# Which TensorE products release the row gathers of a graph layer: those of the small stages and of the picks, or those of the picks alone

## The chip, the cores and the metric

One Trainium2 chip, one NeuronCore of it. The metric is the device time of the whole kernel in microseconds (us). The kernel before takes 1808.46 us, the median of three runs (1806.99 to 1809.7).

## The reference, cut to what matters

200,000 edges, sorted by their target node, join 6,250 nodes of 64 features. Every edge takes the row of its source node, weighs it by nine numbers that a small network makes of its 32 attributes, and the weighted outer products go through `W_tp` and are summed over the edges of each target. A gate made of `node_vec`, the residual and a layer norm end it.

```python
src, dst = edge_index[0], edge_index[1]
w = silu(edge_attr @ W1 + b1) @ W2 + b2                 # 32 -> 64 -> 9, per edge
h_src = features[src]                                   # 64 numbers per edge
msg = einsum('ef,em,fmg->eg', h_src, edge_sh * w, W_tp) # 64 per edge
agg = segment_sum(msg, dst, num_segments=N) / sqrt(E / N)
x = layernorm(x + agg * (1.0 + gamma) + beta)           # gamma, beta from node_vec
```

## The kernel before, in words

The edges lie in 98 blocks (`NBLK`) of 16 tiles of 128 edges. For each block, `hs[g]` (128 x 16 x 64) must be filled with the 128 source rows of each of its tiles. This is done in two ways:

- **Gathers.** An indirect DMA that GpSimd (POOL) issues (line 125) fetches the 128 rows of one tile from DRAM. A block has 12 of them, every fourth block 11, because one tile of it comes row by row over SP's queue (line 143). There are 1148 gathers.
- **Picks.** The other four tiles of a block (three in the first and the last block, five in two of them) are picked out of a copy of `x` that stays in SBUF: VectorE (DVE) makes seven one-hot matrices `hot_k` (line 653), TensorE (PE) multiplies them with the high and the low part of `x` in 14 products into one of three PSUM banks `pxw` (line 668), and DVE takes the right one of seven columns out of it (`xm`, line 678) and sums it into `hs` (line 681). There are 392 picks.

The code is scheduled by hand: a step `i` runs, on PE, pick 0 of block i+1, then the **small stages** (the function `middle`), then picks 1 to 3 of block i+1. The small stages are `hidden(i+2)` (line 594), `second(i+1)` (line 618), in odd steps `project` (line 760), which has ten more products, and `windows(i)` (line 708), which multiplies `hs[i]` with the weighted window matrix `a`. In odd steps two products named `ps` (line 775, function `place`) stand behind the first two and four products of pick 0; ScalarE (ACT) copies half of their bank to `carry` (line 781), DVE adds the other half to the last `carry` (`yt`, line 784), and `second` writes the same PSUM bank next, so it waits for `yt`.

**What sets the times of the gathers.** POOL does nothing but gathers once the setup is done, and takes them in program order. What holds a gather back is a hand-made dependency on a product of PE ("its turn"): in step i the 12 gathers of block i+2 (`LEAD = 2`) are handed out. `beats` sets how many units of PE work a step has and spreads the block's gathers over them evenly; each `beat(units, mm)` behind a product adds that product's units, and a gather that has come due waits for this very product:

```python
def beats(g, units):
    pace.update(g=g, done=0.0, every=units / max(1, len(due[g])))
    pace["next"] = pace["every"] / 2

def beat(units, mm):
    pace["done"] += units
    while due[pace["g"]] and pace["done"] >= pace["next"]:
        gather(pace["g"], len(due[pace["g"]]), mm)
        pace["next"] += pace["every"]
```

A product of a pick counts 1 unit, so a step has 2 * J * 4 = 56 units of picks (J = 7); the small stages count 4.5 (`hidden`), 3.4 (`second`), 12 (`project`) and four times 3.3 (`windows`), and the step's sum is 56 + 21 or 56 + 33. The rows of block i+2 are first read by `windows(i+2)`, two steps later. A gather also waits for the one eight places before it to land.

Of the kernel before, what the change touches and what calls it, by code (L numbers as in the profile page):

```python
# [28 lines left out]
LEAD = 2  # L29
LB = 2  # L30
Q = 5
J = 7
# [20 lines left out]
def picked(g):  # L53

    return Q - 2 if g in (0, NBLK - 1) else Q - (g % 40 != 30)


def tiles(g):
    return min(KB, NT - g * KB)
# [9 lines left out]
def gnn_resnorm_kernel(ctx: ExitStack, tc: tile.TileContext, x, src, dst, dst_row, ea, sh, cn,  # L69
# [18 lines left out]
    with ExitStack() as fast:  # L88
# [10 lines left out]
        def px_next():  # L99

            px_at[0] = (px_at[0] + 1) % px_n[0]
            return pxw[px_at[0]]
# [44 lines left out]
        def beats(g, units):  # L147

            if g < NBLK:
# [5 lines that stand above are left out]
            if not pace:  # L155
                return
# [4 lines that stand above are left out]
# [423 lines left out]
        def hidden(g, act=True, beside=None):  # L584

            e = ea_t.pop(g)
            p1 = psum.tile([P, 2, 4 * P], F32, tag="p1", name=f"p1_{g}")
            p1_t[g] = p1
            if beside:
                beside(p1[:, :, 2 * P:])  # L590
            half = [p1[:, 0, 0:2 * P], p1[:, 1, 0:2 * P], pzw[0][:, 2 * P:], pzw[1][:, 2 * P:]]
            for s in range(2):
                for q in range(4):
                    mm = nc.tensor.matmul(half[q][s * H:(s + 1) * H].rearrange("p (c t e) -> p c t e", c=4, t=2),  # L594
                                     w1bd[q * D:(q + 1) * D, (q % 2) * H:(q % 2 + 1) * H],
                                     e[q * D:(q + 1) * D].rearrange("p (s t c e) -> p s c t e", s=2, t=2, c=4)[:, s],
                                     start=True, stop=True)
            beat(4.5, mm)
            st[g] = work.tile([P, 4, 2 * P], F32, tag="st", name=f"st{g}")
            if act:  # L600
                hidden_act(g)
# [11 lines left out]
        def second(g):  # L613

            s = st.pop(g)
            p2[g] = psum.tile([P, 2, 2 * P], F32, tag="s", name=f"p2_{g}")
            for c in range(KB // 4):
                mm = nc.tensor.matmul(p2[g][c * D:(c + 1) * D, 0, :].rearrange("p (q e) -> p q e", q=4), w2p,  # L618
                                 s[:, :, c * 2 * D:(c + 1) * 2 * D], start=True, stop=True)
            beat(3.4, mm)  # L620
            p2s[g] = work.tile([P, 2 * P], F32, tag="p2s", name=f"p2s{g}")
            nc.scalar.activation(p2s[g], p2[g][:, 0, :], AF.Identity, bias=b2c)  # L622

# [59 lines left out]
        def sums(g):  # L683
            z = zs[g] = zt[:, g % 4]
            if tiles(g) < KB:
                nc.vector.memset(z[:, :, tiles(g):, :], 0.0)
            return z

        def windows(g, k0s=None, last=None):

            nk = tiles(g)
            end = g == NBLK - 1
            hsg, ag = hs[g], a[g]
            z = zs[g] if g in zs else sums(g)


            for k0 in range(0, nk, ZT) if k0s is None else k0s:
                n = min(ZT, nk - k0)
                k1 = 0
                if last is not None:  # L700
                    n, k1 = (n, n - 1) if last else (n - 1, 0)
                pz = [pzw[k0 // ZT][:, 0:ZT // 2 * M * W].rearrange("p (k m w) -> p k m w", m=M, w=W)] * 2
                if end and last is not False:
                    pe = px_next()[:, 0:ZT // 2 * M * W].rearrange("p (k m w) -> p k m w", m=M, w=W)
                    pz = [pe if last else pz[0], pe]
                for k in range(k1, n):
                    v = k % 2
                    mm = nc.tensor.matmul(pz[v][v * F:(v + 1) * F, k // 2].rearrange("p m w -> p (m w)"),  # L708
                                          hsg[:, k0 + k, :], ag[:, k0 + k].rearrange("p m w -> p (m w)"),
                                          start=True, stop=True)  # L710
                    if k % 4 == 3:
                        beat(3.3, mm)
                    if k0 + k == 0:

                        for d in hs_dma.pop(g)[(g not in SPG):]:
                            tc.add_manual_dep(mm.ins, d.ins.name, mybir.DependencyInfo(
                                mybir.DependencyClass.Sync, mybir.DependencyReason.DATA), reason="rows of the group")
                for v in range(2):
                    for h in range(2):
                        k = k1 + (v - k1) % 2  # L720
                        if k >= n:
                            continue
                        copy = nc.vector.tensor_copy if last is False else nc.scalar.copy
                        copy(  # L724
                            z[h * F:(h + 1) * F, 0:5 - h, k0 + k:k0 + n:2, :].rearrange("p m k w -> p k m w"),
                            pz[v][v * F:(v + 1) * F, k // 2:(n + 1 - v) // 2, h:M:2, :])
# [19 lines left out]
        def project(q, pt=None):  # L746


            gs = pair(q)
            z = [zs.pop(g).rearrange("p c k w -> p c (k w)") for g in gs]  # L750
            if len(gs) == 1:
                pr = pt[0:KW, 0:F]
                for c in range(5):
                    nc.tensor.matmul(pr, z[0][:, c], wtc2[:, c, :], start=(c == 0), stop=(c == 4))
                return lambda: halves(q, pr.unsqueeze(1)), None
            if pt is None:
                pt = psum.tile([P, 2, 4 * P], F32, tag="p1", name=f"pt{q}")[:, 0, 0:KW]
            for c in range(5):
                for h in range(2):
                    mm = nc.tensor.matmul(pt[h * F:(h + 1) * F], wtc2[:, c, :], z[h][:, c], start=(c == 0), stop=(c == 4))  # L760
            beat(12, mm)
            rt = work.tile([P, KW], F32, tag="rt", name=f"rt{q}")

            def turn(rp):
                nc.tensor.transpose(rp, rt, ident)  # L765
                return lambda: halves(q, rp.rearrange("p (g f) -> p g f", g=2))

            return lambda: nc.scalar.copy(rt, pt), turn
# [82 lines left out]
        with tc.manual_schedule(), tc.tile_pool(name="temp", bufs=1) as temp:  # L851
# [7 lines left out]
            for i in range(1, NBLK):  # L859
# [13 lines left out]
                    tables.pop()()  # L873
                while stores:
                    stores.pop(0)()
                beats(i + LEAD, 2 * J * picked(i + 1) + (21 if i % 2 == 0 else 33))
                more = []
                if i + 2 < NBLK:
                    more = [lambda: hots(i + 2, 0, 2)]
# [289 lines left out]
```

## Time and profile before

| | before |
|---|---|
| median of three runs | 1808.46 us |
| the profiled execution, as a whole | 1810.38 us |
| its span, first to last instruction | 1808.5 us |
| mean granted TensorE clock | 0.953 |
| PE, DVE, POOL, ACT busy | 88%, 69%, 60%, 28% |
| products of the picks (line 668) | 5488 |
| gathers (line 125) | 1148, 948 ns each |

The profile's page lists busy times by engine and by line, and each group's idle time with what ended it. The chain of work goes back from the last instruction to what released it at each step; "issue" in it is time in which an engine waited for nothing that the profile shows. The timeline gives single instructions: start, duration, engine, line, output <- input, and in brackets the idle time before it and what ended it. The view by stretches gives, for each stretch of time, its length, each engine's busy time with the number of instructions that touch the stretch, and the granted clock of TensorE.

### The profile page before, as it was taken

How to read it: one execution, taken by the hardware profiler on the slowest of the kernel's cores; microseconds unless marked ns; L12 is line 12 of the kernel's file. 1: busy time of each engine (PE TensorE's matmuls, PEld its weight loads, DVE VectorE, ACT ScalarE, POOL GpSimd, SP SyncE). 2: the span in 40 equal slices, each digit the busy share in tenths (PEclk: the TensorE clock that was granted, in tenths of full speed). 3: DMA queues.
4: the chain of work that ended last, by engine and by line, in shares of the span. 5: the costliest groups of instructions: out<-in, count | busy, mean ns of one | idle time of the engine just before them, and what ended most of it. 6: DMA issues, size and time to landing. Idle time of an engine off the chain costs nothing.

```text
span 1808.5 us, 38434 instructions
## 1 busy us (share of the span) xinstructions
PE 1588.4 (88%) x12330; PEld 1338.5 (74%) x12330; DVE 1252.2 (69%) x2249; ACT 512.8 (28%) x1435; POOL 1090.0 (60%) x1157
## 2 busy tenths in 40 slices
PE   5888989899989988988899888988989899888988
PEld 4777878677767777777777777777877677776876
DVE  6677777667667677676776777767767666667676
ACT  3322323232223132323231323232313232222232
POOL 6566566566666666666666666666666666665662
PEclk8899999999999999999999999999999999999999
DMA  5411122112112212122112111211122112211210
GB/s 164 95 46 48 47 71 49 46 49 71 46 49 47 70 49 48 48 69 48 47 47 68 46 47 45 69 45 47 46 66 48 45 46 50 63 47 46 67 24 18
DMA packets 89767, 98.89 MB, mean 55 GB/s; under 512 B 36548, under 2 KB 51094, under 8 KB 89558
## 3 DMA queue, kind: packets, MB, share of 16 engines
q0 software_dynamic: 36736, 37.69, 10.9%
q1 hardware_dynamic: 52246, 57.06, 10.3%
q8 instruction: 100, 1.64, 0.4%
q10 hardware_dynamic: 576, 1.61, 0.2%
q14 instruction: 109, 0.89, 0.2%
HBM read 94.50 MB, written 1.75 MB: 53 GB/s over the span
## 4 chain that ended last, share of the span: by engine, by line
PE 81%; issue 11%; DVE 6%; DMA 1%; another core or an unknown queue 1%; ACT 0%; SPq 0%; POOL 0%; DVEq 0%; ACTq 0%; POOLq 0%
PE pxw L668 59%; PE pzw L708 8%; PE p L760 5%; PE p L618 4%; PE p L594 2%; DVE xm L678 2%; DVE hs L681 1%; PE ps L775 0%; PE p L790 0%; PE p L813 0%; DVE hot_k L653 0%; DMA hs<-in_x_dram,src_i 0%; DVE mean L978 0%; PE p L765 0%
## 5 line engine op out<-in xcount | busy, mean ns | idle before, releaser
L125 POOL DMA_INDIRECT hs<-in_x_dram,src_i x1148 | 1088.8, 948 | 694.7 <-PE pxw L668 224.7
L668 PE MATMUL pxw<-xs_w,hot_k 128*128 128x448 f32 x5488 | 1184.4, 371 | 34.0 <-issue 20.8
L668 PEld LDWEIGHTS pxw<-xs_w,hot_k 128*128 128x128 f32 x5488 | 1030.7, 191 | 136.6 <-issue 51.5
L678 DVE SCALAR_TENSOR_TENSOR xm<-li,jl,pxw 128x448 f32<-128x448 f32 x392 | 265.7, 678 | 418.0 <-PE pxw L668 324.8
L653 DVE TENSOR_TENSOR hot_k<-kr,pxw 128x896 fp32r<-128x896 f16 x385 | 407.1, 1078 | 0.0
L724 ACT COPY ztw<-pzw 64x140 f32<-64x140 f32 (+1 forms) x778 | 208.9, 269 | 155.9 <-PE pxw L668 81.7
L681 DVE TENSOR_REDUCE hs<-xm 128x64 f32<-128x448 f32 x392 | 243.1, 620 | 13.8 <-issue 0.3
L622 ACT ACTIVATE p2s<-p,b2c 128x256 f32<-128x256 f32 x98 | 46.4, 473 | 718.0 <-remote 261.2
L708 PE MATMUL pzw<-a,hs 128*64 128x63 f32 x3116 | 160.0, 246 | 65.6 <-issue 62.8
L708 PEld LDWEIGHTS pzw<-a,hs 128*64 128x64 f32 x3116 | 138.9, 157 | 102.3 <-issue 97.0
L618 PE MATMUL p<-st,w2p 128*32 128x256 f32 x784 | 86.5, 403 | 72.1 <-issue 47.0
L638 DVE TENSOR_TENSOR a<-oh,p 128x1008 f32<-128x1008 f32 x98 | 117.9, 1203 | 3.3
L760 PE MATMUL p<-ztw,wtc 128*64 128x112 f32 x940 | 89.0, 322 | 33.2 <-issue 32.1
L760 PEld LDWEIGHTS p<-ztw,wtc 128*64 128x64 f32 x940 | 67.6, 172 | 67.6 <-issue 67.4
L618 PEld LDWEIGHTS p<-st,w2p 128*32 128x32 f32 x784 | 20.4, 109 | 123.3 <-issue 93.3
L609 ACT ACTIVATE st<-pzw,b1c 128x256 f32<-128x256 f32 x196 | 82.3, 470 | 3.6 <-PE pxw L668 1.7
L605 ACT ACTIVATE st<-p,b1c 128x512 f32<-128x512 f32 x98 | 67.0, 683 | 28.9 <-PE pzw L708 11.5
L781 ACT COPY carry<-ps 128x128 f32<-128x128 f32 x48 | 12.4, 258 | 208.7 <-PE pzw L594 93.9
L594 PE MATMUL pzw<-ea,w1bd 32*64 32x256 f32 x784 | 67.0, 399 | 1.0 <-issue 0.9
L594 PE MATMUL p<-ea,w1bd 32*64 32x256 f32 x784 | 66.1, 400 | 0.0
L629 DVE STREAM_TRANSPOSE p<-p2s 128x256 f32<-128x256 f32 x98 | 44.4, 453 | 10.9 <-issue 7.8
L633 DVE TENSOR_TENSOR p<-p,sh 128x72 f32<-128x72 f32 x196 | 47.2, 241 | 6.7
(176 smaller groups left out, 508.3 us busy)
## 6 DMA issues: line engine op xcount, KB each, us to landing
hs<-in_x_dram SPq DMA_DIRECT2D x2944, 0.2 KB
ea<-in_ea_dram SPq DMA_DIRECT2D x48, 512.0 KB
hs<-in_x_dram,src_i POOLq DMA_INDIRECT x1148
kr<-kd SPq DMA_DIRECT2D x48, 320.0 KB
sh<-in_sh_dram SPq DMA_DIRECT2D x49, 144.0 KB
cb<-cn_d SPq DMA_DIRECT2D x12, 128.0 KB
out_dram<-o SPq DMA_DIRECT2D x23, 64.0 KB
dst_i<-in_dst_dram SPq DMA_DIRECT2D x1, 768.0 KB
```

The lines of the kernel that those rows point to most:

```text
L125: d = nc.gpsimd.indirect_dma_start(out=hs[g][:, t - g * KB, :], out_offset=None, in_=x, in_offset=bass.IndirectOffsetOnAxis(ap=src_i[:, t: ...
L594: mm = nc.tensor.matmul(half[q][s * H:(s + 1) * H].rearrange("p (c t e) -> p c t e", c=4, t=2), w1bd[q * D:(q + 1) * D, (q % 2) * H:(q % 2 ...
L609: nc.scalar.activation(st[g][:, 2 + q], pzw[q][:, 2 * P:], AF.Silu, bias=b1c)
L618: mm = nc.tensor.matmul(p2[g][c * D:(c + 1) * D, 0, :].rearrange("p (q e) -> p q e", q=4), w2p, s[:, :, c * 2 * D:(c + 1) * 2 * D], start= ...
L638: nc.vector.tensor_mul(a[g], oh_t.pop(g)[:, :, None, :].to_broadcast([P, KB, M, W]), sw.unsqueeze(3).to_broadcast([P, KB, M, W]))
L653: nc.vector.tensor_tensor(hot_k[g, t], keys[:, t, None, :].to_broadcast([P, J, P]), n_p.unsqueeze(2).to_broadcast([P, J, P]), op=ALU.is_equal)
L668: mm = nc.tensor.matmul(px.rearrange("p f l -> p (f l)"), hot_k[g, t][:, h, :], xs[i][:, h].rearrange("p f l -> p (f l)"), start=(h == 0 a ...
L678: nc.vector.scalar_tensor_tensor(xm, li[:, None, :].to_broadcast([P, F, J]), jl[:, c:c + 1], px, op0=ALU.is_equal, op1=ALU.mult)
L681: read_by[g, t] = nc.vector.tensor_reduce(hs[g][:, tiles(g) - q + t, :], xm, AX.X, ALU.add)
L708: mm = nc.tensor.matmul(pz[v][v * F:(v + 1) * F, k // 2].rearrange("p m w -> p (m w)"), hsg[:, k0 + k, :], ag[:, k0 + k].rearrange("p m w ...
L724: copy(z[h * F:(h + 1) * F, 0:5 - h, k0 + k:k0 + n:2, :].rearrange("p m k w -> p k m w"), pz[v][v * F:(v + 1) * F, k // 2:(n + 1 - v) // 2 ...
L760: mm = nc.tensor.matmul(pt[h * F:(h + 1) * F], wtc2[:, c, :], z[h][:, c], start=(c == 0), stop=(c == 4))
```

## The change

The four calls of `beat` in the small stages are taken out, so that only the products of the picks count, and the step's sum of units is that of the picks alone. A step's 12 gathers now come due every 56/12 = 4.67 products of picks, three in each pick, and none comes due between pick 0 and pick 1. Nothing else is different: the same gathers in the same order, the same picks.

```diff
@@ hidden
-            beat(4.5, mm)
@@ second
-            beat(3.4, mm)
@@ windows
-                    if k % 4 == 3:
-                        beat(3.3, mm)
@@ project
-            beat(12, mm)
@@ the loop over the steps
-                beats(i + LEAD, 2 * J * picked(i + 1) + (21 if i % 2 == 0 else 33))
+                beats(i + LEAD, 2 * J * picked(i + 1))
```

No instruction changes its place on any engine; what moves is the product whose count a gather waits for. In the built program, POOL's gathers of block 49 (`hs49`; `DMASW` stands for the landing of the eighth gather before it, `PE` for a product) are before:

```order
L125 DMA hs49_11695<-in_x_dram,src_i_60 128x64 [waits DMASW1_49,DVE_49,PE_49]
L125 DMA hs49_11695<-in_x_dram,src_i_60 128x64 [waits DMASW2_49,PE_49]
L125 DMA hs49_11695<-in_x_dram,src_i_60 128x64 [waits DMASW3_49,PE_49]
L125 DMA hs49_11695<-in_x_dram,src_i_60 128x64 [waits DMASW4_49,PE_49]
L125 DMA hs49_11695<-in_x_dram,src_i_60 128x64 [waits DMASW5_49]
L125 DMA hs49_11695<-in_x_dram,src_i_60 128x64 [waits DMASW6_49,PE_49]
```

and with the change:

```order
L125 DMA hs49_11695<-in_x_dram,src_i_60 128x64 [waits DMASW1_49,DVE_49,PE_49]
L125 DMA hs49_11695<-in_x_dram,src_i_60 128x64 [waits DMASW2_49,PE_49]
L125 DMA hs49_11695<-in_x_dram,src_i_60 128x64 [waits DMASW3_49,PE_49]
L125 DMA hs49_11695<-in_x_dram,src_i_60 128x64 [waits DMASW4_49,PE_49]
L125 DMA hs49_11695<-in_x_dram,src_i_60 128x64 [waits DMASW5_49,PE_49]
L125 DMA hs49_11695<-in_x_dram,src_i_60 128x64 [waits DMASW6_49,PE_49]
```

The queue is the same. The fifth gather, which came due together with the fourth at the end of `project`, has a product of its own to wait for. Which products these are does not stand in the rows: before, the first two of this block wait for products 4 and 12 of pick 0, the third for the last of `second`, the fourth for the last of `project`, the sixth for the twelfth of the sixteen of `windows`, and the others for products of picks 1 to 3; with the change the first three wait for products 3, 7 and 12 of pick 0, and the fourth to the twelfth for products 3, 8 and 12 of picks 1, 2 and 3.

## The prediction

> **What bounds the kernel now.** I read the page first, for the engines and the costly groups.
>
> ```profile
> PE 1588.4 (88%) x12330; PEld 1338.5 (74%) x12330; DVE 1252.2 (69%) x2249; ACT 512.8 (28%) x1435; POOL 1090.0 (60%) x1157
> ...
> L125 POOL DMA_INDIRECT hs<-in_x_dram,src_i x1148 | 1088.8, 948 | 694.7 <-PE pxw L668 224.7
> ```
>
> PE is busy for 88% of the span, so the stages in which it is not are worth looking at. POOL's 60% misleads. The timeline of POOL (start, duration, gather, idle time before it) shows why:
>
> ```profile
> 896.16 0.94 POOL L125 DMA_INDIRECT hs<-in_x_dram,src_i  x1 [1.28 <-PE pxw L668]
> 897.41 0.94 POOL L125 DMA_INDIRECT hs<-in_x_dram,src_i  x1 [0.31 <-issue]
> 898.65 0.94 POOL L125 DMA_INDIRECT hs<-in_x_dram,src_i  x1 [0.30 <-PE ps L775]
> 899.90 0.95 POOL L125 DMA_INDIRECT hs<-in_x_dram,src_i  x1 [0.30 <-issue]
> 901.42 0.94 POOL L125 DMA_INDIRECT hs<-in_x_dram,src_i  x1 [0.58 <-PE pzw L594]
> 903.64 0.94 POOL L125 DMA_INDIRECT hs<-in_x_dram,src_i  x1 [1.27 <-remote]
> ```
>
> Gathers follow each other at 897.41 - 896.16 = 1.25 us at the least. 1148 of them take 1435 us of the 1808.5, so POOL can wait for only 373 us in all. The next two views, the chain of waits and the timeline of ACT, show what PE does in the same microseconds.
>
> ```profile
> 897.14 0.12 PE ps L775
> 897.26 2.00 PE pxw L668 x10
> 899.26 0.22 PE p L813 x2
> ...
> 900.10 2.46 issue
> 902.56 0.63 PE p L618 x5
> ```
>
> ```profile
> 901.91 0.27 ACT L781 COPY carry<-ps 128x128 f32<-128x128 f32 x1 [9.75 <-remote]
> ```
>
> `carry` waits for nothing but the second `ps` product, which ended at 897.14 + 0.12 = 897.26. It starts at 901.91, 4.65 us later, with ACT idle all that time. `yt` and the first product of `second` follow at once (902.56), and PE has lost 2.46 us. In these 4.65 us POOL runs gathers at 897.41, 898.65, 899.90 and 901.42, and after the last of them it waits itself. I read this as: **while gathers follow each other closely, the counts that PE's products raise reach the other engines late.** The trace does not name the mechanism; the coincidence is what it shows.
>
> What this does to PE goes by stage. The view of waits, for PE alone (total, times, longest):
>
> ```profile
> PE pzw L708 <- issue: 62.8, 97, 1.2
> PE p L618 <- issue: 47.0, 44, 3.0
> PE p L760 <- issue: 32.1, 52, 1.2
> PE pxw L668 <- issue: 20.8, 56, 1.3
> ...
> PE pzw L708 <- DMA hs<-in_x_dram,src_i: 1.9, 3, 0.8
> ```
>
> 142 us go in the small stages (62.8 + 47.0 + 32.1), only 21 in the picks, which have three PSUM banks and one-hot matrices ahead. The rows themselves are never late: 1.9 us.
>
> Then the view by stretches, restricted to gathers, over 45 odd and 45 even steps: the small stages, and the picks from pick 1 to pick 0 of the next step. Columns: length, POOL's busy time (gathers touching the stretch), clock, DMA. The first stretch and the sum of each answer, in the order odd small stages, even small stages, picks after odd, picks after even:
>
> ```profile
> 135.33:142.81 7.48, 4.21 (x6) 1.00 0.09 19
> ...
> sum 344.03, POOL 201.94; mean POOL 4.49
> ```
>
> ```profile
> 155.01:158.68 3.67, 2.00 (x3) 1.00 0.88 290
> ...
> sum 200.51, POOL 106.44; mean POOL 2.37
> ```
>
> ```profile
> 142.81:155.01 12.20, 7.57 (x9) 1.00 0.19 38
> ...
> sum 560.97, POOL 352.64; mean POOL 7.84
> ```
>
> ```profile
> 158.68:170.42 11.74, 7.58 (x9) 1.00 0.13 25
> ...
> sum 529.04, POOL 337.72; mean POOL 7.50
> ```
>
> Divided by 45, and POOL's time by 0.948 us: odd small stages 7.65 us with 4.73 gathers, even ones 4.46 us with 2.49, picks after odd 12.47 us with 8.27, after even 11.76 us with 7.92. A pair of steps takes 36.3 us and 23.4 gathers. In the picks a gather costs 12.47 / 8.27 = 1.51 and 11.76 / 7.92 = 1.49 us.
>
> How long a small stage takes follows how many gathers fall into it. The shortest and one of the longest even ones, then the same for odd ones:
>
> ```profile
> 1683.98:1686.52 2.54, 1.08 (x2) 1.00 0.62 222
> 1717.54:1724.45 6.91, 4.02 (x6) 0.86 0.11 23
> 1298.10:1303.26 5.16, 2.42 (x4) 1.00 0.17 35
> 1332.14:1342.16 10.02, 6.32 (x7) 0.90 0.11 23
> ```
>
> Even: (6.91 - 2.54) us for (4.02 - 1.08) / 0.948 = 3.1 gathers, 1.4 us each. Odd: 4.86 us for 4.1, 1.2 us each. Part of that is the other way round (a longer stage holds more gathers), so 1.2 is the upper bound of what one gather more costs there, and zero the lower.
>
> **The change part by part.** *The pace.* A product of a pick takes 0.205 us:
>
> ```profile
> 909.62 9.66 PE pxw L668 x47
> ```
>
> Before, gathers come due every 77/12 = 6.4 products (1.31 us) or 89/12 = 7.4 (1.52 us). With the change it is 4.67 products, 0.96 us, below POOL's 1.25. So POOL falls behind during the picks: 12 come due in 56 products (11.5 us), and it can do 11.5 / 1.25 = 9.2 at its very best, 7.7 at the 1.5 us that a gather costs there now. Between 2.5 and 4 gathers are then left when the small stages start, against 4.73 and 2.49 that ran in them before. *The taken beats* cost nothing on PE: the products stay.
>
> *How many gathers run in the small stages.* At today's cost per gather in the picks, 11.7 - 7.92 = 3.8 are left for the odd small stages (0.95 fewer) and 11.7 - 8.27 = 3.4 for the even ones (0.94 more). At 1.2 us each that is -1.1 and +1.1: zero per pair. I take zero; the bounds are in the rivals.
>
> *Where they run.* Before, POOL was served piecemeal there and paused for each release (1.27 us before 903.64). Now all that is left is due already, and runs in one piece from the first moment: 3.6 x 1.25 = 4.5 us, and about 1 us more until counts come through, going by the 1.27 us pause. PE wants `yt` 0.85 us into an odd small stage (899.26 to 900.10 in the chain). If the count of `ps` comes at a random moment of the 5.5 us, PE waits on average 2.75 - 0.85 = 1.9 us; now it is 47.0 / 44 = 1.07. That is +0.8 us per pair, between 0 (it slips through early) and +3.6 (it comes at the very end). In both kinds of stage `windows` waits for the last pick's sum in `hs`, raised one pick earlier: I take +0.3, an estimate from the 62.8 / 97 = 0.65 us of its waits now.
>
> *The clock.* After the gap of 2.46 us the granted clock is halved for 3.41 us (clock after POOL's count):
>
> ```profile
> 872.55:903.27 30.72, 27.57 (x196) 23.77 (x196) 20.78 (x37) 8.48 (x27) 18.74 (x20) 1.00 0.22 57
> 903.27:906.68 3.41, 3.36 (x31) 2.55 (x33) 3.38 (x5) 0.58 (x2) 1.88 (x2) 0.50 0.06 15
> ```
>
> That costs 3.41 / 2 = 1.7 us of PE's work each time. If the longer gaps bring it in every fifth odd step more, it is 1.7 / 5 = +0.3 per pair; the ends are 0 and +1.7, and I take the low one's side because most gaps stay near 2 us. Over the span the mean is
>
> ```profile
> core 0: 1808.5 us, clock 0.953
> ```
>
> The Trainium skill, "TensorE: Matmul & The Clock Gate", section "Why this matters for your kernels", has the clock fall only after PE idles for more than about 3 us between bursts; here 2.46 us were enough, so the trace decides. By the page's rule the term would be 0 and the sum 14 us less.
>
> *What is won.* After a longer drain, POOL enters the picks after an odd step without a backlog. These take 12.47 us against 11.76 after an even one; I give back most of that difference, -0.6, between 0 and -0.71.
>
> *Landing.* A gather waits in order, so all later ones wait behind it; PE's `windows` needs them. They end at worst 3.8 x 1.25 = 4.8 us into the next step and are read a step later, some 13 us away: nothing. Gone, that cover would show as L708 waiting for DMA, today 1.9 us, and cost one gather's 1.25 us per place that it comes late. SP, ACT and DVE issue what they did.
>
> Sum: 0 + 0.8 + 0.3 + 0.3 - 0.6 = +0.8 us per pair, 48 pairs: +38 us on the profiled span of 1808.5, which equals the median of the runs (1808.46; the profiled execution as a whole was 1810.38). **1847 us.**
>
> **The rivals.** *Faster.* The picks take the gathers at 1.25 us instead of 1.5, because POOL never lacks a release there: 11.7 / 1.25 = 9.3 fit, and 2.4 are left. Then the odd small stages lose 2.3 gathers, the even ones none: -2.3 x 1.2 = -2.8 us per pair at the upper bound, half of that as a middle: -67 us, 1741. It decides from the point where the picks hold more than about 8.1 gathers. For it: PE loses only 21 us in the picks. Against: POOL's idle time goes mostly with releases that come late, and these come from PE through the same late counts. 0.3.
>
> *The clock falls in every small stage.* One run of gathers at the start of each leaves PE idle long enough everywhere: +1.7 for each of 96 instead of about a third of them, 64 x 1.7 = +109 us on top of nothing else, 1917. For it: the halved stretch above. Against: the even stage has no `carry`. 0.1.
>
> *Nothing happens.* POOL is busy at its own rate either way, and the places don't matter: 1808. The Trainium skill, "TensorE: Matmul & The Clock Gate", section "The cost: per-tile semaphore tail", has the increments of successive products pass one after the other at some 26 ns each. By that rule a dozen of them are through in 0.3 us, no count could be late by microseconds, and where the gathers stand would not touch PE. The 4.65 us of `carry` speak against it. 0.1.
>
> **How the numbers follow.** The forecast has 0.5, the rivals 0.3, 0.1 and 0.1. A measurement tells about 0.2% from no change (the three runs spread by 0.15%). Slower: 0.5 and 0.1, 0.6; same 0.1; faster 0.3. The range takes in the bounds of the forecast (0 for `carry` and the clock gives -0.3 per pair, 1794; +3.6 for `carry` is 1981, cut where one in ten is left above) and half of the faster rival: 1765 to 1915. Own range of the forecast: 1812 to 1900.
>
> **What would show it.** Right: in the picks gathers at 1.25 us in runs longer than the six of the timeline; in the small stages three to four in one piece and then an idle POOL until product 3 of pick 1; L618's wait on PE above 60 us, `carry` later; a lower mean clock than 0.953. Wrong: small stages shorter in sum than 7.65 + 4.46 us per pair, a POOL with more than 8.3 gathers per stretch of picks, waits at L708 and L760 that shrink. If L668 waits much more than 21 us, the picks had less cover than I say.

## The result, and the profile after

The changed kernel takes 2021.11 us, the median of four runs (2014.76 to 2026.2), against 1807.72 us for the kernel before beside it (four runs): a ratio of 1.118, with a 95% interval of 1.114 to 1.122. The forecast was 1847, in a range from 1765 to 1915: the sign was right, and the loss is 213 us instead of 38.

One thing must be known for what follows: the kernel before, unchanged, took 1808 to 1833 us on most occasions and 1455 us on some (of two occasions with the same chip number in the records one was of each kind), so every experiment stands beside the kernel before as it was measured on that occasion.

The page of the changed kernel, with the rows that answer to those shown of before:

```profile
PE 1712.4 (85%) x12330; PEld 1444.5 (71%) x12330; DVE 1254.6 (62%) x2249; ACT 506.2 (25%) x1435; POOL 1087.4 (54%) x1157
...
L125 POOL DMA_INDIRECT hs<-in_x_dram,src_i x1148 | 1086.1, 946 | 914.1 <-PE pxw L666 594.2
L666 PE MATMUL pxw<-xs_w,hot_k 128*128 128x448 f32 x5488 | 1238.3, 386 | 9.8 <-ACT pxw L369 8.5
...
L706 PE MATMUL pzw<-a,hs 128*64 128x63 f32 x3116 | 214.3, 275 | 161.6 <-issue 158.2
...
L756 PE MATMUL p<-ztw,wtc 128*64 128x112 f32 x940 | 101.0, 303 | 84.4 <-issue 82.6
...
L617 PE MATMUL p<-st,w2p 128*32 128x256 f32 x784 | 75.8, 398 | 33.7 <-issue 13.6
```

The lines moved by the calls taken out: L708 of before is L706 here (`windows`), L760 is L756 (`project`), L618 is L617 (`second`), L668 is L666 (picks). The gathers cost what they cost (1086.1 us, 946 ns each). POOL's idle time went from 694.7 to 914.1 us, +219, and that is the whole growth of the span (2024.4 - 1808.5 = 216). What it waits for is new too: 594.2 us for products of picks, against 224.7.

The view of waits, for PE alone (total, times, longest), tells where PE stands:

```profile
PE pzw L706 <- issue: 158.2, 231, 1.9
PE p L756 <- issue: 82.6, 114, 1.7
...
PE p L617 <- issue: 13.6, 21, 1.4
```

In `second` the waits fell, from 47.0 to 13.6 us; in `windows` and `project` they rose, from 94.9 (62.8 + 32.1) to 240.8. "issue" means that the profile shows nothing that PE waits for. The rows are not late: all of L706's idle time that is not "issue" is 161.6 - 158.2 = 3.4 us.

One even stage of `windows` in the timeline shows PE held and then POOL without work (the lines of PE and POOL alone; start, duration, what, idle time before it):

```profile
1028.13 0.21 PE L706 MATMUL pzw<-a,hs 128*64 128x63 f32 x1 [0.15 <-issue]
1028.49 0.94 POOL L125 DMA_INDIRECT hs<-in_x_dram,src_i  x1 [0.30 <-issue]
1028.86 0.30 PE L706 MATMUL pzw<-a,hs 128*64 128x63 f32 x2 [0.51 <-issue]
1029.74 0.94 POOL L125 DMA_INDIRECT hs<-in_x_dram,src_i  x1 [0.30 <-issue]
1030.30 0.22 PE L706 MATMUL pzw<-a,hs 128*64 128x63 f32 x1 [1.14 <-issue]
1030.99 0.95 POOL L125 DMA_INDIRECT hs<-in_x_dram,src_i  x1 [0.30 <-issue]
1031.01 0.21 PE L706 MATMUL pzw<-a,hs 128*64 128x63 f32 x1 [0.50 <-issue]
1031.73 0.28 PE L706 MATMUL pzw<-a,hs 128*64 128x63 f32 x2 [0.50 <-issue]
1033.16 1.58 PE L706 MATMUL pzw<-a,hs 128*64 128x63 f32 x25 [1.15 <-issue]
1034.67 2.63 PE L666 MATMUL pxw<-xs_w,hot_k 128*128 128x448 f32 x8
1036.43 0.94 POOL L125 DMA_INDIRECT hs<-in_x_dram,src_i  x1 [4.49 <-PE pxw L666]
```

While POOL runs what was left over from the picks (until 1031.94), PE gets one or two of the 32 passes of `windows` (two for each of its 16 products) through at a time; 1.2 us after the last gather the other 25 go in 1.58 us. By then POOL has nothing due, and it rests 4.49 us until a product of pick 1 releases the next. First PE is held, then POOL starves: two things in series that lay, in part, beside each other before.

The same can be counted over the 90 small stages of the view by stretches below, if gathers less than 0.5 us apart are taken as one run:

| in the small stages | before: time, PE idle in it | after: time, PE idle in it |
|---|---|---|
| inside a run of gathers | 365.5 us, 22% | 410.4 us, 39% |
| up to 1.5 us behind a run | 169.9 us, 44% | 181.3 us, 53% |
| later, with POOL still idle | 9.1 us, 2% | 126.0 us, 8% |

So PE is held inside a run and for some 1.5 us behind it, and goes freely only after that; that third kind of time, in which POOL does nothing, hardly existed before.

The same stretch in the view by stretches (length, PE, PEld, DVE, ACT and POOL busy, granted clock, DMA):

```profile
1028.13:1033.16 5.03, 1.22 (x8) 0.81 (x7) 3.57 (x5) 0.00 (x0) 2.90 (x4) 0.98 0.15 30
1033.16:1034.67 1.51, 1.51 (x25) 1.38 (x25) 0.10 (x1) 1.19 (x3) 0.00 (x0) 0.50 0.00 1
1034.67:1036.43 1.76, 1.76 (x7) 1.60 (x6) 1.66 (x6) 1.68 (x8) 0.00 (x0) 0.53 0.00 1
```

PE is busy for 1.22 of the 5.03 us, and the clock is halved behind them and stays so in the first products of pick 1, though no single gap was longer than 1.15 us. Over the span:

```profile
core 0: 2024.4 us, clock 0.897
```

PE's busy time grew from 1588.4 to 1712.4 us, 124.0 us for the same 12330 products, and its idle time from 220.1 to 312.0, 91.9 us: together the 216 us of the span. The idle time is the waits on nothing (+145.9 at `windows` and `project`, -33.4 at `second`, -20.8 in the picks: 92 us). The busy time is mostly the clock: 2024.4 x 0.103 = 209 us of it were not granted, against 1808.5 x 0.047 = 85, again 124 us more. That these two agree is partly chance: of the 124 us not granted some 106 fell where PE was busy, counted over the halved stretches of both traces; the rest of the busy time fits the passes that come alone (0.21 us each above).

Last, the view by stretches, restricted to gathers, over the same 45 odd and 45 even steps as before: the sums for odd small stages, even small stages, picks after odd and picks after even ones.

```profile
sum 373.55, POOL 162.60; mean POOL 3.61
...
sum 344.07, POOL 167.03; mean POOL 3.71
...
sum 535.36, POOL 322.60; mean POOL 7.17
...
sum 589.99, POOL 344.48; mean POOL 7.66
```

| per step | before, us (gathers) | after, us (gathers) | longer by | POOL without a gather, before and after |
|---|---|---|---|---|
| odd small stages | 7.65 (4.73) | 8.30 (3.82) | +0.66 | 3.16, 4.69 |
| even small stages | 4.46 (2.49) | 7.65 (3.92) | +3.19 | 2.09, 3.93 |
| picks after odd | 12.47 (8.27) | 11.90 (7.58) | -0.57 | 4.63, 4.73 |
| picks after even | 11.76 (7.92) | 13.11 (8.09) | +1.35 | 4.25, 5.46 |

The last column is the length less POOL's busy time, over 45. The pair grew by 4.63 us, 48 pairs by 222; in the small stages POOL's time without a gather grew by 3.4 us a pair.

### The profile page after: what moved, and what is told of

It reads as the page before. It is cut to its first block, busy times and chain, and to the rows that moved or that the text cites. A ratio compares the mean times of both kernels' runs of the same rounds, so it can differ in the third digit from the quotient of the medians.

```text
span 2024.4 us, 38461 instructions
## 1 busy us (share of the span) xinstructions
PE 1712.4 (85%) x12330; PEld 1444.5 (71%) x12330; DVE 1254.6 (62%) x2249; ACT 506.2 (25%) x1435; POOL 1087.4 (54%) x1157
## 2 busy tenths in 40 slices
DMA packets 89767, 98.89 MB, mean 49 GB/s; under 512 B 36548, under 2 KB 51094, under 8 KB 89558
## 5 line engine op out<-in xcount | busy, mean ns | idle before, releaser
L125 POOL DMA_INDIRECT hs<-in_x_dram,src_i x1148 | 1086.1, 946 | 914.1 <-PE pxw L666 594.2
L666 PE MATMUL pxw<-xs_w,hot_k 128*128 128x448 f32 x5488 | 1238.3, 386 | 9.8 <-ACT pxw L369 8.5
L666 PEld LDWEIGHTS pxw<-xs_w,hot_k 128*128 128x128 f32 x5488 | 1097.7, 203 | 101.1 <-ACT pxw L369 8.7
L706 PE MATMUL pzw<-a,hs 128*64 128x63 f32 x3116 | 214.3, 275 | 161.6 <-issue 158.2
L706 PEld LDWEIGHTS pzw<-a,hs 128*64 128x64 f32 x3116 | 174.1, 182 | 218.0 <-issue 214.3
L756 PE MATMUL p<-ztw,wtc 128*64 128x112 f32 x940 | 101.0, 303 | 84.4 <-issue 82.6
L756 PEld LDWEIGHTS p<-ztw,wtc 128*64 128x64 f32 x940 | 67.7, 157 | 123.9 <-issue 123.1
L617 PE MATMUL p<-st,w2p 128*32 128x256 f32 x784 | 75.8, 398 | 33.7 <-issue 13.6
L594 PE MATMUL pzw<-ea,w1bd 32*64 32x256 f32 x784 | 80.1, 399 | 6.1 <-issue 5.9
L497 DVE TENSOR_SCALAR gam<-p 128x64 f32<-128x64 f32 x49 | 11.0, 224 | 117.0 <-ACT st L604 107.0
L617 PEld LDWEIGHTS p<-st,w2p 128*32 128x32 f32 x784 | 17.9, 108 | 80.9 <-issue 50.2
```

What stands on the lines that cost most here:

```text
L125: d = nc.gpsimd.indirect_dma_start(out=hs[g][:, t - g * KB, :], out_offset=None, in_=x, in_offset=bass.IndirectOffsetOnAxis(ap=src_i[:, t: ...
L666: mm = nc.tensor.matmul(px.rearrange("p f l -> p (f l)"), hot_k[g, t][:, h, :], xs[i][:, h].rearrange("p f l -> p (f l)"), start=(h == 0 a ...
```

## The experiments

**Four ways of counting, on an occasion without the hold-up** (one on which the kernel before took 1455 us). The kernel before, with all counts of the small stages halved (half), with all doubled (double), with only those of `hidden` and `second` (first_two), and with only those of `project` and `windows` (last_two). In the expectations the run theory says that the unbroken run of left-over gathers costs, the carry theory that the late count for `carry` does. Here is first_two, and the others likewise:

```diff
-                    if k % 4 == 3:
-                        beat(3.3, mm)
...
-            beat(12, mm)
...
-                beats(i + LEAD, 2 * J * picked(i + 1) + (21 if i % 2 == 0 else 33))
+                beats(i + LEAD, 2 * J * picked(i + 1) + 7.9)
```

> The small stages' units are halved (2.25, 1.7, 1.65, 6; step sums 56 + 10.5 or 16.5), so about half as many gathers come due by their products. If what costs is the unbroken run of left-over gathers that meets the small stages, the time lies between the two kernels, 1870 to 1960, and the clock between 0.90 and 0.95. If the cost sets in only once none comes due there, it stays within 1% of 1808. If late counts for the carry are the cause, L617/L618 waits grow with the time.

> The small stages' units are doubled (9, 6.8, 6.6, 24; sums 56 + 42 or 66): 5 to 6.5 of 12 gathers come due by products of the small stages, and in the picks one every 1.7 to 2.1 us. If a backlog at the start of the small stages is all that costs, this is as fast as before or faster, 1760 to 1808. If each gather in a small stage costs about 1.2 us wherever it comes due, 1.5 to 2 more of them per step make it 1950 to 2050.

> Only hidden and second release gathers beside the picks (sum 56 + 7.9). Windows and project release none, and these are the lines whose waits grew (95 and 50 us). Run theory: most of the loss stays, 1930 to 2010. Carry theory: the count of ps is wanted between hidden and second, so gathers released there are what matters, and most of the loss goes, below 1870.

> Only project and windows release gathers beside the picks (sum 56 + 13.2 or 25.2). Run theory: the backlog at the start is smaller and gathers come due only as windows goes on, so most of the loss goes: 1820 to 1890. Carry theory: the loss before second stays, above 1930.

Measured: 1454.76, 1454.68, 1454.8 and 1454.59 us, beside 1455.20 for the kernel before: ratios of 0.9994 to 0.9996, each interval from 0.998 to 1.001. None of the theories was tested by it, but something else shows. The page of first_two there:

```profile
PE 1436.3 (99%) x12330; PEld 1259.3 (87%) x12330; DVE 1244.6 (86%) x2249; ACT 504.7 (35%) x1435; POOL 1089.2 (75%) x1157
...
L125 POOL DMA_INDIRECT hs<-in_x_dram,src_i x1148 | 1088.0, 948 | 351.9 <-DMA hs<-in_x_dram,src_i 156.2 <-issue 93.6 <-PE pxw L668 64.9
...
L708 PE MATMUL pzw<-a,hs 128*64 128x63 f32 x3116 | 110.2, 223 | 1.3 <-issue 1.1 <-DMA hs<-in_x_dram,src_i 0.2
```

The gathers take the same 948 ns and run back to back at 1.25 us; PE is busy for 99% and waits 1.1 us at `windows`. So a run of gathers does not of itself hold PE up. What makes it do so on the other occasions, none of the runs shows: the kernel's trace here and its trace on an occasion with the hold-up, further below, have the same 89767 DMA packets and 98.89 MB. The sums by stretches of this run (odd, then even small stages) give the length of an unhindered stage:

```profile
sum 156.11, POOL 118.73; mean POOL 2.64
...
sum 125.57, POOL 94.96; mean POOL 2.11
```

They are 156.11 / 45 = 3.47 us and 2.79 us. An estimate of two things in series, the unhindered stage and the gathers that fall into it at 1.25 us each, gives 3.47 + 3.82 x 1.25 = 8.2 and 2.79 + 3.92 x 1.25 = 7.7 us for the changed kernel, which took 8.30 and 7.65. For the kernel before it gives 9.4 and 5.9, where 7.65 and 4.46 were taken: there some of the two overlaps, with the change hardly anything does. The estimate leaves out the halved clock and the 1.5 us behind a run, so that it comes out to within 0.1 us is partly chance.

**Fewer gathers, or none on POOL.** All other experiments but the four named at their places were on occasions where the kernel before took 1832 to 1833. Eight of 12 gathers in a step, with the change's releases and with those of before; and POOL's gathers replaced by plain DMAs of fixed rows on SP's queue. In all three the 2944 single rows of SP are left out, and `windows` reads another tile for what is not fetched.

```diff
@@ eight gathers
-            due[g] = list(range(g * KB + (g in SPG), g * KB + tiles(g) - picked(g)))
+            due[g] = list(range(g * KB + 4, g * KB + tiles(g) - picked(g)))
@@ plain DMAs
-                d = nc.gpsimd.indirect_dma_start(
...
+                d = nc.sync.dma_start(hs[g][:, t - g * KB, :], x[0:P, :])
```

> Four of a block's twelve gathers are left out (windows reads four other tiles in their place) and the rows over SP's queue too; eight come due in the picks alone, every 7 products (1.44 us), so POOL can keep up and nothing is left over. Run theory: the small stages are free of gathers, shrink towards 2.5 and 5.2 us, the clock stays at 0.97 or above, and the time falls to 1500 to 1600. If taking the beats out of the small stages costs by itself (late counts, the place of the waits), it stays slower than the kernel with eight gathers spread over all products.

> The same eight gathers, spread over picks and small stages as before. Run theory: two to three of them fall into each small stage, and it is slower than the kernel with eight in the picks alone by 1 us or more per step, 1600 to 1720. Rival: spread is better whatever the number, so it is the faster of the two.

> The changed kernel with every gather replaced by a plain DMA of SP's queue that moves as many rows of the same size (always the same 128 rows of x), released by the same products; the rows over SP's queue for every fourth block are left out (windows reads another tile). POOL issues nothing in the loop. If POOL's own work on a gather holds PE up, the waits of L706 and L756 go to a few us and the time to 1480 to 1600. If the landing of the rows is what holds PE up, they stay, and the time stays above 1900.

Measured, beside 1831.74: 1468.12 (ratio 0.801, 0.799 to 0.803), 1462.31 (0.798, 0.795 to 0.800) and 1460.65 (0.797, 0.795 to 0.799). The waits on nothing at `windows` and `project` with eight gathers and the change's releases, and the engines without gathers on POOL:

```profile
PE pzw L706 <- issue: 3.9, 8, 1.1
...
PE p L756 <- issue: 1.4, 2, 0.9
```

```profile
PE 1438.4 (99%) x12330; PEld 1261.7 (86%) x12330; DVE 1240.6 (85%) x2249; ACT 505.0 (35%) x1435; POOL 1.3 (0%) x9
```

With eight gathers PE is all but free, and faster than the 1500 to 1600 of the run theory. Spreading them is worth 6 us, with intervals that overlap; the run theory had it slower, at 1600 to 1720. Without gathers on POOL nothing is held up (1461, a little below the 1480 of its expectation), although as many tiles of rows land in the same buffers. So PE suffers from POOL's indirect gathers, and not from the mere landing of as many rows. Which part of a gather does it is not shown: the plain DMAs differ in the queue, in the addressing, and in fetching the same 128 rows each time.

**What SP's rows add.** The changed kernel without SP's single rows, and with eight gathers but with SP's rows (each leaves those tiles out).

> The changed kernel with all its gathers, without the 2944 single rows that SP's queue fetches for every fourth block (windows reads another tile there). It parts two suspects that the kernels with eight gathers and with SP's plain DMAs took away together. If POOL's gathers alone hold PE up, it stays at 1950 to 2030. If the single rows of SP's queue hold PE up, alone or only beside the gathers, it falls to 1455 to 1600 and the clock to above 0.98.

> The changed kernel with four gathers of each block left out (windows reads other tiles in their place) and with the single rows over SP's queue kept. If it is the number of gathers, it runs in 1460 to 1480 as without the rows. If the single rows are what matters, L706 and L756 wait as much as in the changed kernel per gather, and it takes 1650 or more.

Measured, beside 1833.0: 1961.08 (1.070, 1.066 to 1.073) and 1501.81 (0.819, 0.817 to 0.822). By the ratios, taking the rows away brings the changed kernel from 11.8% above the kernel before (which has them) to 7.0%, and the one with eight gathers from 18.1% below it to 19.9%: they make it worse, and are not its cause. What the kernel before would take without them was not measured. The second kernel's 1502 lies between its two expectations. From eight gathers to 12 (779 to 1148 in all), with the rows, the ratio rises from 0.819 to 1.118; of 1833 us that is 548 us for 369 gathers, 1.49 us each, somewhat more than the 1.25 us in which they follow each other. I read it so that eight fit into the picks, and what does not fit is paid in full; between eight and 12 nothing was measured where it could show.

**All at once.** The changed kernel, all 12 gathers released by the first product of pick 1.

```diff
-                    beat(1, mm)
+                    if pace and (t, h, i) == (1, 0, 0):
+                        gather(pace["g"], 1, mm)
```

> All 12 gathers of a step come due at the first product of pick 1 and follow each other without a pause: 15 us, of which 11.5 lie beside the picks, so 2 to 3 are left for the small stages. Run theory: fewer left over than the 3.5 of the changed kernel, so faster than 2021, 1850 to 1980, if the picks bear a run of 9; if products of picks are held up by so long a run too, L666 waits by more than 100 us and it is slower than 2021.

Measured: 2257.81 us beside 1831.74, a ratio of 1.232 (1.227 to 1.237). The waits of PE:

```profile
PE p L594 <- issue: 164.0, 161, 2.4
PE pzw L594 <- issue: 143.4, 143, 2.5
```

The run of 12 x 1.25 = 15 us covers the picks and reaches into the next stage, and PE stands in `hidden`, the first of it, for 307 us in all; the view has no wait on nothing at `windows` any more. Its place moves with the run of gathers. The clock is 0.843. Both expectations failed: it is not faster, and the picks (L666) wait on nothing for 7.3 us, not 100; what both missed is that the run reaches past the picks into `hidden`.

**Which counts matter.** The first experiment's kernels again, where the kernel before takes over 1800 us.

> Of the small stages only `hidden` and `second` count (a step is 56 + 7.9 units), so a gather comes due every 5.3 products of a pick and none in `project` or `windows`; work and rows as in the kernel before. The time is looked at where the kernel before takes above 1800 us. Theory A (what costs is the backlog of gathers that runs in one piece when the small stages begin, 3.5 gathers with the change, about none before): 56 / 5.3 = 10.5 come due in the picks, which take 8, so the backlog is about 2.5 and the loss lies between the two kernels, +80 to +160 us on the kernel before. Rival B (it matters that none comes due at `windows` and `project`, where PE does not issue): the loss is the whole of the change's, +180 to +220 us. Rival C (the first counts, at `hidden` and `second`, are the ones that matter): within 40 us of the kernel before.

> Of the small stages only `project` and `windows` count (a step is 56 + 13.2 or 56 + 25.2 units), so a gather comes due every 5.8 or 6.8 products of a pick, and none in `hidden` or `second`; work and rows as in the kernel before. The time is looked at where the kernel before takes above 1800 us. Theory A (the backlog at the start of the small stages): 9.7 and 8.3 come due in the picks, which take about 8, so a backlog of about one: +10 to +60 us on the kernel before. Rival B (what counts is that gathers come due at `windows` and `project`): as the kernel before, within 20 us. Rival C (the counts at `hidden` and `second` are the ones that matter): +180 to +220 us.

> The kernel before with the units of the four counts in the small stages doubled (a step is 56 + 42 or 56 + 66 units); work and rows as before. A gather comes due every 8.2 or 10.2 products of a pick, so 6.9 and 5.5 of 12 in the picks, and 5 to 6.5 within the small stages. The time is looked at where the kernel before takes above 1800 us. Theory A, read narrowly (only the backlog that stands when the small stages begin costs): no backlog, so 20 to 60 us faster than the kernel before. Rival H (gathers back to back within the small stages cost as well, wherever they came due: POOL needs 1.25 us for each, five take 6.3 us of a stage of 3.5): slower by 30 to 150 us, so that the kernel before stands near the best of its kind.

Measured: first_two 1931.87 beside 1832.87 (1.055, 1.053 to 1.058); last_two 1842.62 beside 1832.87 (1.006, 1.004 to 1.008); double 1838.26 beside 1831.51 (1.004, 1.002 to 1.005). PE's waits in `windows` and `project` of the three, in this order:

```profile
PE pzw L708 <- issue: 148.7, 226, 1.3
PE p L758 <- issue: 72.1, 100, 1.2
```

```profile
PE pzw L706 <- issue: 75.9, 121, 1.2
PE p L758 <- issue: 55.7, 82, 1.2
```

```profile
L708 PE MATMUL pzw<-a,hs 128*64 128x63 f32 x3116 | 177.0, 237 | 115.0 <-issue 108.4 <-DMA hs<-in_x_dram,src_i 4.1
...
L760 PE MATMUL p<-ztw,wtc 128*64 128x112 f32 x940 | 67.4, 276 | 6.7 <-issue 5.8
```

The sums are 220.8, 131.6 and 114.2 us, against 94.9 before and 240.8 with the change: nearly the order of the times, though not their size (double waits longer than the kernel before and takes as long; first_two waits 20 us less than the changed kernel and loses 99 us on the kernel before where the change loses 213). In first_two less of the clock is lost: 0.925, 1925.4 x 0.075 = 144 us, against 209.

So the counts at `project` and `windows` keep nearly all of the loss away (0.6% is left of 11.8%), and the counts at `hidden` and `second` alone somewhat more than half of it (5.5% is left). Rival B hit last_two and missed first_two, where it wanted the whole loss; rival C missed both. Theory A hit the number of first_two and just missed that of last_two, but the backlog by itself does not part them. Counting the releases against the gathers in the traces, it is 2.3 at the start of the small stages before, 2.7 in last_two, 3.5 with the change, and in first_two 2.1, or 2.8 with the gather that the last product of pick 0 releases 0.17 us into the stage: next to last_two's 2.7, and first_two loses 99 us where last_two loses 10. Nor did double gain by more counts, or lose by what its rival H said.

One rival is left. The place of the counts and the number of gathers that come due in the picks changed together: by the paces, 10.5 of 12 in first_two against 9.7 and 8.3 in last_two, where the picks take about eight. No run that fell on an occasion with the hold-up parts the two. What the kernels before, last_two and double share is that gathers come due at the end of the stage, by its own products. That PE goes on while POOL pauses for them is not borne out by the count above: in the first 1.5 us of a pause PE is idle more often than inside a run, before the change as after it.

**Held for a time, or a toll for each instruction?** The changed kernel, each product of `windows` given twice.

```diff
-                    mm = nc.tensor.matmul(pz[v][v * F:(v + 1) * F, k // 2].rearrange("p m w -> p (m w)"),
+                    for _ in range(2):
+                        mm = nc.tensor.matmul(pz[v][v * F:(v + 1) * F, k // 2].rearrange("p m w -> p (m w)"),
...
```

> The changed kernel, in which each product of `windows` is given twice in a row with the same operands and the same output (16 products more in a step, nothing left out, the gathers as with the change). The products more cost 32 passes of 0.036 us in 97 steps, 113 us, where nothing holds PE up. Theory E (PE is held at the windows for a stretch of time, until the backlog of gathers has been run): the waits on nothing at the windows stay near 158 us and the time rises by 90 to 130 us on the changed kernel, to some 2110 to 2150. Rival F (each instruction that PE is given pays a toll while gathers run, 158 us for the 32 passes and 32 weight loads of a step): the waits double to about 310 us, and with the clock the time rises by 250 us or more, to 2270 at least. Rival G (the picks, which come next, have slack, so that more work at the windows hides): under 60 us more.

> The changed kernel, in which each product of `windows` is given twice (16 products more in a step, nothing left out). Where nothing held PE up (a chip on which the kernel before took 1456), this cost 93 us on it. The time is looked at where the kernel before takes above 1800 us, beside the changed kernel's 2021. Theory E (PE is held at the windows for a stretch of time, until the backlog of gathers has been run): the waits on nothing at the windows stay near 158 us, and the time rises by 80 to 130 us, to some 2100 to 2150. Rival F (each instruction that PE is given pays a toll while gathers run): the waits there double to about 310 us, and the time rises to 2270 at least. Rival G (the picks, which come next, have slack): under 60 us more.

The first fell on an occasion without the hold-up: 1548.76 beside 1456.07 (1.064, 1.062 to 1.065), the plain cost of the products, 93 us (if the changed kernel takes there what the kernel before does, as the other spacings did). The second took 2153.04 beside 1831.51 (1.179, 1.174 to 1.185). By the ratios that is 1.179 / 1.118 = 1.055 of the changed kernel, about 110 us. Its waits:

```profile
PE pzw L707 <- issue: 132.2, 216, 1.3
PE p L757 <- issue: 89.6, 122, 1.9
```

With twice as many instructions the waits at `windows` are 132.2 us instead of 158.2, and the new products cost what they cost unhindered, plus some of it at half clock: PE's busy time is 1826.1 us, 113.7 more than with the change, and its idle time 322.7 against 312.0. A toll for each instruction (310 us of waits, 2270) is refuted, and so is that they hide. PE is held for a stretch of time, and the work behind it adds in full, as it does where two things are in series.

**More than those.** Three runs fell on occasions without the hold-up: the halved counts again, 10 gathers in a step (two tiles left out), and the kernel before with a fifth pick in place of a gather in each odd block.

```diff
-    return Q - 2 if g in (0, NBLK - 1) else Q - (g % 40 != 30)
+    return Q - 2 if g in (0, NBLK - 1) else Q - (g % 40 != 30 and (g % 2 == 0 or g < 5))
```

> The units of the four counts in the small stages are halved (a step is 56 + 10.5 or 56 + 16.5 units); work and rows as in the kernel before. A gather comes due every 5.5 or 6.0 products of a pick: 10.1 and 9.3 of 12 in the picks, which take about 8. Theory A (the backlog that stands when the small stages begin is what costs; measured so far: 9.0 due in the picks on average cost +10 us, 10.5 cost +99, 12 cost about +200): 9.7 on average, +30 to +70 us on the kernel before. Rival D (every count in a small stage helps alike, so half of them gives half of the loss): +90 to +120 us.

> The changed kernel with 10 gathers in a step instead of 12; what it leaves out: two tiles of a block are not fetched (two others are taken twice), all else as with the change. The time is looked at where the kernel before takes above 1800 us. With 12 gathers it took 2021 (a step of 20.5 us), with 8 it took 1502. Theory K (two things in series in the small stages: PE is held until POOL has worked off what is left from the picks, then POOL has nothing due while PE does its products): a gather comes due every 5.6 products, about 1.7 are left when a small stage begins; a step is 11.5 us of picks, 3.4 of small stages and 1.7 x 1.25 = 2.1 of holding up, 17.0 us, with 97 steps and 30 to 60 for the clock some 1650 to 1740 us. Rival L (a threshold: below the number that POOL can do in the picks at its own pace nothing is lost): 1490 to 1530. Rival M (the cost is in proportion to the number alone, (2021 - 1502) / 4 = 130 us for each): 1740 to 1790.

> The kernel before with a fifth pick in place of a gather in each odd block (48 gathers fewer, 48 picks more; nothing left out, the counts in the small stages as before). A pick more is 14 products of 0.205 us, 2.87 us of PE, 141 us in all; a gather less is worth 1.5 us where POOL is what the step waits for, 74 us in all. The time is looked at where the kernel before takes above 1800 us. Theory K (a step of the kernel before is 12 gathers of 1.5 us, PE fits in beside them): 1.0 % to 4 % faster than the kernel before. Rival N (PE's time in the small stages and the gathers do not overlap, so that PE's products add in full): 2 % to 8 % slower. On a chip without the hold-up both give 5 % to 10 % slower.

Measured: 1455.55 beside 1456.07 (1.000, 0.999 to 1.001); 1454.07 beside 1455.5 (0.999, 0.998 to 1.000); 1581.93 beside 1455.5 (1.087, 1.085 to 1.089). The last is the expected price of the picks where PE is the bound, 126 / 46 = 2.75 us each (46 blocks have a fifth pick, not the 48 of the expectation). What these three do where PE is held up stays open, and with it the onset between eight and 12 gathers, and whether trading gathers for picks would beat both kernels there. No version that does the whole work was faster than the kernel before.

## Why the prediction was wrong

- **What bounds the kernel: half right.** That gathers close together hold PE back was read rightly from `carry`, and the runs with eight gathers and without gathers on POOL show it. But the trace of before was read as counts that reach others late; what costs most is PE itself, which issues next to nothing at `windows` and `project` while POOL runs and just behind, with no count in the profile that it waits for. The row was there, 62.8 us on "issue" at L708 with 97 waits, larger than the 47.0 at L618 on which the working was built.
- **How many gathers run in the small stages: right for odd, low for even.** Forecast 0.95 fewer and 0.94 more; measured 0.91 fewer and 1.43 more. Their number per pair changed by 0.5 and cannot make 4.63 us, not even at the 1.4 us each that the even stages gave, which the forecast left out when it called 1.2 the upper bound.
- **Where they run, +0.8 for the late `carry`: failed.** L617's wait fell by 33.4 us, -0.7 per pair. This term alone made the forecast's sum positive (0.3 + 0.3 - 0.6 is zero), so that the sign came out right is luck. It was foreseen that what is left runs in one piece; the piece now stands in the way of `windows` and `project` and not of `second`.
- **The windows' wait, +0.3: the step that failed most.** At `windows` it is 158.2 - 62.8 = 95.4 us over 48 pairs, +2.0; at `project`, for which the sum has no term and no reason for that, 82.6 - 32.1 = 50.5 us, +1.05; together 145.9 us, +3.0. The forecast took it for a wait on the last pick's sum, something that comes late once, and priced it by half of today's mean wait. What the runs showed in its place: PE is held while the run lasts and some 1.5 us behind it, and then POOL has nothing due. The piece that is left was also compared with the wrong number: 2.5 to 4 gathers at the start of a stage stand against a backlog of 2.3 before, and not against the 4.73 and 2.49 that ran in it. Giving `windows` and `project` their counts back takes nearly all of the loss away; whether by their place or by what no longer comes due in the picks stays open.
- **The clock, +0.3 between 0 and +1.7: mis-sized.** 124 us over 48 pairs is +2.6, and the 106 us of it in which PE was busy are +2.2, both beyond its upper end. The forecast tied the half clock to single gaps of 2.46 us; the timeline above has it after a row of gaps none of which is longer than 1.15 us. The trace of before already had that: without setup and end it has 35 halved stretches, and ahead of 19 of them no gap reaches 1.2 us. What they share is how little PE was busy in the 3.41 us ahead of them: 20 to 62%, with a median of 46%; with the change it is 74 stretches, 13 to 74% and 39%. Cut on the grid on which the halved stretches lie, 3.41 us at full clock that were followed by 3.41 more had PE busy for at least 52% before and 56% after. The rule of the Trainium skill, "TensorE: Matmul & The Clock Gate", section "Why this matters for your kernels" (a fall only after more than about 3 us of idling), would have given nothing here. The better guide is the section "A second HAM failure mode: psum-queue depth-cycling" of the same page of the Trainium skill: short idles between groups of products, when they are frequent enough, make the clock swing too. The trace agrees with that one: PE busy for 1.22 of 5.03 us, then 0.50.
- **What is won in the picks after odd steps, -0.6: right** (-0.57). **In the picks after even steps nothing was forecast:** they lost 1.35 us. The half clock that begins at `windows` lasts into them, as the last of the three stretches shows (0.53); by the traces the clock not granted in such a stretch of picks rose from 0.15 to 1.68 us.
- **Landing, 0: right.** The idle time of L706 that is not "issue" is 161.6 - 158.2 = 3.4 us.
- **The rivals.** *Faster* had the picks take more gathers at 1.25 us: they took 7.58 and 8.09, no more than before. *Nothing happens* is what the occasions at 1455 us show for other spacings, and there alone; the changed kernel itself was not run there. *The clock falls in every small stage* named the other part of the loss; it had no hold-up beside it and so gave 1917.

## What to carry to other kernels

Spreading an engine's work evenly over another's long stages is not the same as spreading it over time: look at what each engine has due in the short stages, and in which order it gets it. If one engine is held while another runs, work that is all due before a short stage puts the two in series there; spread over the stage, as before the change, they overlap in part. A row on "issue", where the engine waits for nothing that the profile shows, is priced by what else runs at that time and not by its mean.

## What the runs showed of the hardware

- The same program took 1455 us on some occasions and 1808 to 1833 on others, with gathers of 946 to 948 ns in both: in the one PE is busy for 99% (first_two, 1454.8 us), in the other it stands still in the small stages while POOL's gathers run back to back and some 1.5 us behind them (first_two again, 86%, 1931.87 us). No run shows what decides between the two.
- In a held stretch PE issues one or two passes about every 0.71 us (1030.30, 1031.01, 1031.73 in the timeline), and the picks' products of 0.205 us are hardly touched (9.8 us idle over 5488).
- The clock halves after several gaps of 0.5 to 1.15 us within 5 us in which PE was busy for 1.22 us. In the traces before and after, setup and end left out, the 3.41 us ahead of a halved stretch had PE busy for 13 to 74%, with medians of 46% and 39%, and in none of the 109 cases was there a gap above 3 us.
